# A two-layer graph network on one core: slabs 2 to 6 multiply a folded, re-split hT once in fp16, and the epilogue's operations stand in other steps

## The chip, the cores and the metric

The kernel runs on one core of one Trainium2 chip. The core has five engines, each with an instruction queue of its own that it works off in order: PE multiplies matrices, DVE and ACT work elementwise and read the results of PE out of PSUM, POOL works elementwise on SBUF and issues the large loads, SP issues the small ones. They wait for each other through semaphores. The metric is the time of one execution on the device, in microseconds (us).

## The reference

There are 4096 nodes with 64 features each (x) and a 0/1 matrix adj of 4096 x 4096 with about 16 ones in a row.

```python
# layer 0
support = x @ W0
rank = cumsum(adj, axis=1); deg = rank[:, -1:]
k = minimum(deg, 100)
w = adj * where(rank - (deg - k) > 0, 0.5 ** (k - (rank - (deg - k))), 0)   # the last neighbour counts 1, the one before 1/2, ...
x1 = layernorm(x + w @ support + b0)
# layer 1
deg1 = sum(adj, axis=1) + 1
z = concat([x1, (adj @ x1 + x1) / deg1]) @ W + b1      # W = [Wx; Wn]
o = relu(z)
out = layernorm(x1 + o / max(norm(o), 1e-12))
```

The layer norms have no weights; eps is 1e-5.

## The kernel before, in words

**Tiles.** The host hands over the adjacency transposed and cut into 64 tiles. Tile (g, k) holds the 512 rows of slab g (the destinations) and the 512 columns of chunk k (the sources); it comes as 1 MB of f32 and is written into SBUF as bf16, 512 KB (L105). There are 33 buffers for such tiles. Slab by slab, and within a slab from chunk 7 down to chunk 0, this gives the 64 steps of the main loop (L539 to L576): step 8g is the first of slab g. Eight loads are issued ahead; step i issues load i + 8, on POOL's queue.

**One step, layer 0.** For every tile the neighbours are counted with matmuls against `pick` (`count`, L248), the counts are added up on DVE (cs, L258 or L260), multiplied out to all ranks (`spread`: rep on PE, L266; near on ACT, L268), and turned into exponents v by two times 16 matmuls of 32 x 32 (`weigh`, L278 and L287). ACT makes one half of v into the weights w (L294), DVE the other (L295): the exponent is written as an integer whose bits are a bf16 power of two. PE then sums w times x over the tile (`gather`, acc, L305), one step later. The two halves of v fill PSUM tiles that exist once, so the v of a step waits for both w of the step before. Slabs 0 to 2 count and spread tile by tile; slab 3 first by one and then by two, slab 4 by two, slabs 5 and 6 by four, slab 7 by two, two and four. x is split into a high and a low fp16 half (`xhl`; the low one times 2048), so acc holds 64 rows of high and 64 rows of low sums: hT is [128, 512].

**The epilogue of a slab** runs in the steps of the next slab, spread over them by a table of hooks: `at(i, engine, fn, g)` puts a function at the end of step i on PE, DVE or POOL, ahead of that step's w (ACT), or behind it ("ACT, late"). Counting from the first step of the next slab: `first_hT` copies acc (ACT, L408); step 1 `first_pz`, four fp32 products hT times W0 (L414) and four degree matmuls (L416), and `first_y` (L421, L422); step 2 `first_mv` (mean and variance); step 3 `first_s` (root, ACT) and `first_r`; step 4 `first_x1` (four scalings on DVE, L441); step 5 `first_hi` (ACT, L446) and `first_xl` (DVE, L450); step 6 `first_lo` (ACT, L453), `first_px` (four transposes, PE, L458) and `first_least`; step 7 `first_x1T` (ACT, L461) and `first_pu` (x1 times Wx, eight fp16 matmuls, PE, L468); step 8 `first_c1` (DVE, L473 and L476: bias, times the degree). Functions on one engine and step run in the order of their registration.

**Sums of layer 1.** When a slab's x1hl is ready, adj times x1 can be summed for every tile in SBUF whose chunk that slab is. `jobs` lists 39 tiles that are summed within the loop, four matmuls a step (`some_sums`, QUOTA = 4, L314, into the one bank "acc1"); steps in SAVED make none. A finished job is copied (ACT) or added (DVE) into part (`evict_part`, L334, L337). The buffer of a tile comes free with its sum, so later loads wait on POOL for these sums.

**Other work on the queues.** In slab 0 ACT and POOL split x (`split_x`, L208, L210); POOL prepares the weights (L216 to L227), adds b0 to x (L238) and the identity to the diagonal tiles (`add_self`, L233).

**The tail** (L579 on) does the last slab's layer 0, the sums that are left and layer 1's epilogue in an order written out by hand; PE works through to about 207 us, then DVE, POOL and ACT end the chain.

The order of a step in the loop:

```python
            run(i, ACT)
            load_next()
            run(i, POOL)
            w = weigh(g, k, nr) if i == 0 else None
            for s in share:
                count(*s, s == ahead[0], s == ahead[-1])
            w = w or weigh(g, k, nr)
            run(i, "ACT, late")
            ...
            run(i, PE)
            run(i, DVE)
```

Of the kernel before, what the change touches and what calls it, by code (L numbers as in the profile page):

```python
# [9 lines left out]
F32 = mybir.dt.float32  # L10
BF16 = mybir.dt.bfloat16
FP16 = mybir.dt.float16
# [3 lines left out]
ALU = mybir.AluOpType  # L16
AX = mybir.AxisListType
PE = mybir.EngineType.PE
ACT = mybir.EngineType.Activation
DVE = mybir.EngineType.DVE  # L20
POOL = mybir.EngineType.Pool
SP = mybir.EngineType.SP

P = 128
R = 512
TB = R // P
KB = 4
# [3 lines left out]
W_EXP = 127 - MAX_NEIGH  # L31
LO = 2048.0
W_UP = 256.0
LN_EPS = 1e-5
L2_EPS = 1e-12
QUOTA = 4
SAVED = 23, 26, 28


@with_exitstack  # L40
def adj_resnorm_kernel(
# [23 lines left out]
    nc = tc.nc  # L65
    D = x.shape[2]
    NG, NK = adjT.shape[0], adjT.shape[1]
# [4 lines left out]
    const = ctx.enter_context(tc.tile_pool(name="const", bufs=1))  # L72
# [39 lines left out]
    c1 = const.tile([P, NB, D], F32, name="c1")  # L112
    xp = c1

    def load_xp(k0, k1):
        bs = slice(k0 * KB, k1 * KB)
        nc.sync.dma_start(out=xp[:, bs, :], in_=x_quads[:, bs, :])
# [33 lines left out]
    nc.vector.memset(eps_ln, LN_EPS)  # L151
    ident = epi.tile([P, P], F32, tag="near", name="ident")
    nc.vector.tensor_scalar(ident, dist, 0.0, None, ALU.is_equal)


    has = epi.tile([P, P], BF16, tag="y", name="has")
# [23 lines left out]
    nc.vector.memset(less, -STEP * MAX_NEIGH)  # L180


    wts = const.tile([P, 5 * D], F32, name="wts")
    w0_sb, wn_sb, wx_sb, b1_sb, b0_sb = [wts[:, j * D : (j + 1) * D] for j in range(5)]

    wx_parts = const.tile([P, 2, D], FP16, name="wx_parts")
    part = {}
# [17 lines left out]
    def split_x(k):  # L205

        bs = ts(k, KB)
        nc.scalar.copy(xhl[:, bs, 0:D], xp[:, bs, :])  # L208
        xrs[k] = epi.tile([P, KB, D], F32, tag="z", name=f"xr_{k}")
        nc.gpsimd.tensor_tensor(xrs[k], xp[:, bs, :], xhl[:, bs, 0:D], ALU.subtract)  # L210

# [11 lines left out]
    def prepare_wx():  # L223
        for rows, up in ((slice(0, D), W_UP), (slice(D, P), W_UP / LO)):
            nc.gpsimd.tensor_scalar(wx_sb[rows, :], wx_sb[rows, :], up, None, ALU.mult)
        nc.gpsimd.tensor_copy(wx_parts[:, 0, :], wx_sb)
        nc.gpsimd.tensor_tensor(wx_parts[:, 1, :], wx_sb, wx_parts[:, 0, :], ALU.subtract)  # L227

    def add_self(g):

# [13 lines left out]
    def count(g, k, first, last):  # L244
        if first:
            cnt[g] = ps_m.tile([P, R], F32, tag="m", name=f"cnt_{g}_{k}")
        for q in range(KB):
            nc.tensor.matmul(  # L248
                cnt[g][quarters[q], :],
                lhsT=pick[:, PW - 4 * k : PW - 4 * k + Q],  # L250
                rhs=A[g][k][:, q, :],
                start=first,
                stop=last,
            )
        if last:
            new = one.tile([P, R], BF16, tag="cs", name=f"cs_{g}_{k}")
            if g in cs:
                nc.vector.tensor_tensor(new, cnt[g], cs[g], ALU.add)  # L258
            else:
                nc.vector.tensor_copy(new, cnt[g])  # L260
            cs[g] = new
# [8 lines left out]
    def weigh(g, k, nr):  # L270

        w = wp.tile([P, KB, R], I16, tag="w", name=f"w_{g}_{k}")
        v = [ps_v.tile([P, 2, R], F32, tag="v", name=f"v_{g}_{k}_{i}") for i in range(2)]
        for q in range(KB):
            for e in range(4):
                nc.tensor.matmul(  # L278
                    v[e // 2][quarters[q], e % 2, :],
                    lhsT=tri[quarters[e], :],  # L280
                    rhs=A[g][k][quarters[e], q, :],
                    start=True,
                    stop=False,
                )
        for q in range(KB):
            for e in range(4):
                nc.tensor.matmul(  # L287
                    v[e // 2][quarters[q], e % 2, :],
                    lhsT=mine[quarters[e], 4 * k + q, :],
                    rhs=nr[quarters[e], :],  # L290
                    start=False,
                    stop=True,
                )
        nc.scalar.activation(w[:, 0:2, :], v[0], AF.Relu, bias=less)  # L294
        nc.vector.tensor_scalar(w[:, 2:4, :], v[1], -STEP * MAX_NEIGH, 0.0, ALU.add, ALU.max)  # L295
        return w
# [17 lines left out]
        nc.tensor.matmul(acc, lhsT=x1hl[:, b, :], rhs=A[g][b // KB][:, b % KB, :], start=first, stop=last)  # L314


    jobs = [(0, [0]), (1, [0])]
    jobs += [(2, [0, 1]), (0, [1]), (1, [1])]
    jobs += [(3, [1, 0, 2]), (0, [2]), (1, [2]), (2, [2]), (4, [2, 1, 0, 3])]
    jobs += [(0, [3]), (1, [3]), (2, [3]), (5, [3, 2, 1, 0, 4]), (3, [3, 4])]  # L320
    jobs += [(6, [4, 3, 2, 1, 0, 5]), (4, [4, 5]), (0, [4, 5]), (1, [4, 5]), (2, [4])]
    acc1 = {}

    todo = [(g, k * KB + q, (k, q) == (ks[0], 0), (k, q) == (ks[-1], KB - 1)) for g, ks in jobs for k in ks for q in range(KB)]
# [1 line left out]

    def ready(i, g, b):
        k = b // KB
        return i >= NK * (k + 1) + 7 and i >= when[g, k]

    def evict_part(g):
        acc = acc1.pop(g)
# [62 lines left out]
    def psum(n, m, name, dt=F32):  # L395

        if not banks:
            return ps_m.tile([P, n, m], dt, tag="m", name=name)
        bank = banks.pop(0)
        bank_of[name] = bank  # L400
        view = bank if dt == F32 else bank.bitcast(dt)
        return view[:, 0 : n * m].rearrange("p (n m) -> p n m", m=m)
# [1 line left out]
    bank_of = {}  # L404

    def first_hT(g):
        ep["hT", g] = epi.tile([P, R], F32, tag="hT", name=f"hT0_{g}")
        nc.scalar.copy(ep["hT", g], acc0[g])  # L408

    def first_pz(g):  # L410

# [25 lines left out]

    def first_x1(g):
        mv, y, r = ep["mv", g], ep["y", g], ep["r", g]
        for t in range(TB):  # L440
            nc.vector.tensor_scalar(  # L441
                x1[:, g * TB + t, :], y[:, t, :], mv[:, t, 0:1], r[:, t : t + 1], ALU.subtract, ALU.mult
            )

# [2 lines left out]

    def first_xl(g):
        xl = ep["xl", g] = epi.tile([P, TB, D], F32, tag="z", name=f"xl_{g}")
        nc.vector.tensor_tensor(xl, x1[:, ts(g, TB), :], x1hl[:, ts(g, TB), 0:D], ALU.subtract)  # L450

    def first_lo(g):
        nc.scalar.mul(x1hl[:, ts(g, TB), D : 2 * D], ep["xl", g], LO)  # L453
# [15 lines left out]

    def first_c1(g):  # L470

        t1 = c1[:, ts(g, TB), :]
        nc.vector.scalar_tensor_tensor(  # L473
            t1, ep["pu", g], 1.0 / W_UP, b1_sb.unsqueeze(1).to_broadcast([P, TB, D]), ALU.mult, ALU.add
        )
        nc.vector.tensor_tensor(  # L476
            t1, t1, deg[:, ts(g, TB)].unsqueeze(2).to_broadcast([P, TB, D]), ALU.mult
        )

    hooks = defaultdict(list)  # L480

    def at(i, engine, fn, *args):
        hooks[i, engine].append((fn, args))

    def run(i, engine):
        for fn, args in hooks.pop((i, engine), []):
            fn(*args)

    for k in range(NK):
        i = when[0, k]  # L490
# [6 lines left out]
    for g in range(NG):  # L497
        at(NK * g + 3, POOL, load_x, g)
        at(NK * g + 7, POOL, add_b0, g)
        at(min(NK * g + 12, NS - 2), POOL, add_self, g)  # L500
    for g in range(NG - 1):
        i = NK * (g + 1)
        at(i + 1, PE, first_pz, g)
        at(i + 1, DVE, first_y, g)
        at(i + 2, DVE, first_mv, g)
        at(i + 3, "ACT, late", first_s, g)
        at(i + 3, DVE, first_r, g)
        at(i + 4, DVE, first_x1, g)
        at(i + 5, ACT, first_hi, g)
        at(i + 5, DVE, first_xl, g)  # L510
        at(i + 6, ACT, first_lo, g)
        at(i + 6, PE, first_px, g)
        at(i + 7, ACT, first_x1T, g)
        at(i + 7, PE, first_pu, g)
        at(i + 6, DVE, first_least, g)
        at(i + 8, DVE, first_c1, g)

# [19 lines left out]
    for c, chunk in enumerate(chunks):  # L539
        ahead = chunks[c + 1] if c + 1 < len(chunks) else []  # L540

        shares = [[]] * (len(chunk) - 1) + [ahead]
        nr = near[chunk[0][0]]
        for (g, k), share in zip(chunk, shares):
            i = when[g, k]
# [4 lines that stand above are left out]
            w = weigh(g, k, nr) if i == 0 else None  # L550
            for s in share:
                count(*s, s == ahead[0], s == ahead[-1])
            w = w or weigh(g, k, nr)
            run(i, "ACT, late")
            if i == 0:
                warm(4)
            n_todo = len(todo)
            done = some_sums(i, 0 if i in SAVED else QUOTA)
            half = 0
            if share and share[-1] == ahead[-1]:  # L560
                if held is not None and len(todo) == n_todo:

                    half = KB // 2
                    gather(*held, 0, half)
                spread(*ahead[-1])
            if i == 0:
                warm(3)
            if done is not None:
                evict_part(done)
            if held is not None:  # L570
                gather(*held, half)
            held = (g, k, w)
            if g > 0 and k == NK - 1:
                first_hT(g - 1)
            run(i, PE)
            run(i, DVE)  # L576
# [317 lines left out]
```

## Time and profile before

| | us |
|---|---|
| median of 3 runs (236.61 to 238.28) | 236.71 |
| the profiled execution | 236.54 |
| its span, first to last instruction | 234.4 |
| PE busy | 210.6 (90%) |
| DVE busy | 180.1 (77%) |
| ACT busy | 136.6 (58%) |
| POOL busy | 82.6 (35%) |
| adjacency loads: 64 of 512 KB, median from issue to landing | 16.6 |
| main loop: first L278 of step 0, first L278 of step 63 | 12.4, 189.1 |

Busy times are sums over an engine's instructions; overlapping matmuls count once. The mean granted clock of PE is 0.978, and the page's row for it shows full speed in nearly every slice. A timeline's row has start, length, engine, line, operation, output<-input and shapes; "x16" are 16 instructions in one row, and in brackets stands how long the engine was idle before and what ended it. A waits row has the engine and line that waited, what for, the sum in us, how often, and the longest.

### The profile page before, as it was taken

What the parts mean: (1) busy time and instruction counts of PE and PEld (TensorE: products, weight loads), DVE (VectorE), ACT (ScalarE), POOL (GpSimd) and SP (SyncE); (2) the same over time, 40 slices, a digit from 0 to 9 for tenths busy, and PEclk for the clock granted to TensorE, in tenths of its full rate; (3) what the DMA queues carried; (4) which work ended last, traced back from release to release, by engine and by line L of the source; (5) the groups of instructions that cost most, each with busy time, mean ns of one, the idle gap of its engine ahead of it and who ended that gap; (6) DMA issues with size and microseconds to landing.
All of it is one profiled execution on the core that took longest, in us unless ns stands there. A gap on an engine that the chain in (4) does not pass through costs nothing.

```text
span 234.4 us, 7427 instructions
## 1 busy us (share of the span) xinstructions
PE 210.6 (90%) x3129; PEld 97.0 (41%) x3172; DVE 180.1 (77%) x461; ACT 136.6 (58%) x205; POOL 82.6 (35%) x158
## 2 busy tenths in 40 slices
PE   7689979889998999999999999999999999999920
PEld 2223324234434343453345334533443345676810
DVE  5459897987897779779857985597579776499983
ACT  6068877688678765665655555555565551232684
POOL 8334583432531330312231143114441000069970
PEclk9799999999999999999999999999999999999985
DMA  6999999999999999999999999999980000000013
GB/s 201 212 212 219 208 214 212 222 215 215 218 216 212 216 219 214 214 216 212 219 213 204 201 190 191 168 174 172 212 167 3 0 3 0 3 0 3 25 45 112
DMA packets 11985, 37.34 MB, mean 159 GB/s; under 512 B 1328, under 2 KB 3504, under 8 KB 11952
## 3 DMA queue, kind: packets, MB, share of 16 engines
q0 software_dynamic: 9216, 33.56, 73.4%
q1 hardware_dynamic: 2736, 3.31, 4.6%
q8 instruction: 25, 0.41, 0.6%
q14 instruction: 8, 0.07, 0.1%
HBM read 69.37 MB, written 1.05 MB: 300 GB/s over the span
## 4 chain that ended last, share of the span: by engine, by line
PE 50%; DVE 7%; POOL 4%; ACT 3%; issue 2%; ACTq 0%; POOLq 0%
PE acc L305 13%; PE acc_part L314 12%; PE v L278 6%; PE cnt L248 4%; PE v L287 3%; PE pz L414 2%; ACT u L788 2%; DVE w L295 2%; POOL scratch L774 2%; PE vb L314 2%; POOL scratch L805 2%; PE rep L266 1%; PE va L757 1%; DVE x L441 1%; PE va L314 1%
## 5 line engine op out<-in xcount | busy, mean ns | idle before, releaser
L294 ACT ACTIVATE w<-v,less 128x1024 int16<-128x1024 f32 x64 | 71.2, 1113 | 48.5 <-PE v L287 36.2
L295 DVE TENSOR_SCALAR w<-v 128x1024 int16<-128x1024 f32 x64 | 78.2, 1221 | 18.6 <-PE v L287 17.2
L105 POOL DMA_DIRECT2D a<-in_adjT_dram x64 | 35.4, 554 | 97.0 <-PE rep L266 35.4
L305 PE MATMUL acc<-w,xhl 128*128 128x512 bf16 x240 | 66.1, 379 | 2.1 <-issue 1.1
L314 PE MATMUL acc_part<-a,x1hl 128*128 128x512 bf16 x132 | 37.3, 381 | 2.1 <-issue 1.4
L305 PEld LDWEIGHTS <-xhl 128*128 128x128 f16 x256 | 23.0, 98 | 32.6 <-issue 9.3
L268 ACT ACTIVATE near<-rep,most 128x512 bf16<-128x512 f32 x40 | 27.3, 682 | 8.3 <-PE rep L266 8.2
L314 PEld LDWEIGHTS <-x1hl 128*128 128x128 f16 x224 | 18.5, 98 | 31.2 <-issue 13.8
L278 PE MATMUL v<-a,tri 32*32 32x512 bf16 x1024 | 28.6, 384 | 0.5 <-ACT w L294 0.5
L287 PE MATMUL v<-near,mine 32*32 32x512 bf16 x1024 | 27.8, 376 | 0.0
L248 PE MATMUL cnt<-a,pick 128*32 128x512 bf16 x256 | 21.4, 389 | 5.8 <-DMA a<-in_adjT_dram 4.2
L258 DVE TENSOR_TENSOR cs<-cnt,cs 128x512 bf16<-128x512 f32 x32 | 21.9, 684 | 5.4 <-PE cnt L248 5.1
L278 PEld LDWEIGHTS <-tri 32*32 32x32 bf16 x1024 | 9.6, 87 | 19.5 <-issue 18.7
L774 POOL TENSOR_TENSOR scratch<-scratch,power 128x4 f32<-128x4 f32 (+1 forms) x5 | 6.4, 1278 | 29.5 <-DVE scratch L776 29.4
L266 PE MATMUL rep<-cs,further 128*128 128x512 bf16 x40 | 15.4, 385 | 1.0 <-DVE cs L258 1.0
L248 PEld LDWEIGHTS <-pick 128*32 128x32 bf16 x256 | 5.9, 94 | 20.8 <-issue 12.4
L233 POOL TENSOR_TENSOR a<-a,ident_b 128x128 bf16<-128x128 bf16 x32 | 12.7, 429 | 0.1
L287 PEld LDWEIGHTS <-mine 32*32 32x32 bf16 x1024 | 10.5, 87 | 2.8 <-issue 2.6
L788 ACT ACTIVATE u<-u,scratch 128x64 f32<-128x64 f32 x27 | 9.8, 429 | 2.2 <-POOL scratch L807 2.1
L260 DVE CAST cs<-cnt 128x512 bf16<-128x512 f32 x8 | 5.5, 692 | 6.9 <-PE cnt L248 6.8
L446 ACT CAST x1hl<-x 128x256 f16<-128x256 f32 x8 | 3.2, 405 | 11.1 <-DVE x L441 9.2
L771 ACT ACTIVATE u<-u 128x256 f32<-128x256 f32 (+1 forms) x5 | 2.5, 502 | 12.1 <-DVE u L760 12.1
(134 smaller groups left out, 245.0 us busy)
## 6 DMA issues: line engine op xcount, KB each, us to landing
a<-in_adjT_dram POOLq DMA_DIRECT2D x64, 512.0 KB, 16.6
c<-in_x_quads_dram SPq DMA_DIRECT2D x2, 512.0 KB, 4.5
x<-in_x_dram SPq DMA_DIRECT2D x8, 128.0 KB, 7.6
out_dram<-u SPq DMA_DIRECT2D x8, 128.0 KB, 1.7
wts<-in_weights_dram SPq DMA_DIRECT2D x1, 160.0 KB, 7.1
```

The source lines that it names most:

```text
L105: nc.gpsimd.dma_start(out=a, in_=adjT[g, k])
L248: nc.tensor.matmul(cnt[g][quarters[q], :], lhsT=pick[:, PW - 4 * k : PW - 4 * k + Q], rhs=A[g][k][:, q, :], start=first, stop=last,)
L258: nc.vector.tensor_tensor(new, cnt[g], cs[g], ALU.add)
L266: nc.tensor.matmul(pr, lhsT=further, rhs=cs[g], start=True, stop=True)
L268: nc.scalar.activation(near[g], pr, AF.Relu, bias=most, scale=-1.0)
L278: nc.tensor.matmul(v[e // 2][quarters[q], e % 2, :], lhsT=tri[quarters[e], :], rhs=A[g][k][quarters[e], q, :], start=True, stop=False,)
L287: nc.tensor.matmul(v[e // 2][quarters[q], e % 2, :], lhsT=mine[quarters[e], 4 * k + q, :], rhs=nr[quarters[e], :], start=False, stop=True,)
L294: nc.scalar.activation(w[:, 0:2, :], v[0], AF.Relu, bias=less)
L295: nc.vector.tensor_scalar(w[:, 2:4, :], v[1], -STEP * MAX_NEIGH, 0.0, ALU.add, ALU.max)
L305: nc.tensor.matmul(acc0[g], lhsT=xhl[:, b, :], rhs=w[:, q, :].bitcast(BF16), start=(k, q) == (NK - 1, 0), stop=(k, q) == (0, KB - 1),)
L314: nc.tensor.matmul(acc, lhsT=x1hl[:, b, :], rhs=A[g][b // KB][:, b % KB, :], start=first, stop=last)
L788: nc.scalar.activation(o[:, t, :], y[:, t, :], AF.Identity, bias=off[:, t : t + 1], scale=r[:, t : t + 1])
```

## The change

For slabs 2 to 6 (`HALVED`) hT's low half is folded into its high half in f32 (`half_sum`, DVE), the sum is split again into an fp16 high part (`half_high`, ACT), what is left of it (`half_rest`, DVE) and that as fp16 low part (`half_low`, ACT), both in x1T. Eight fp16 matmuls of 128 columns (`half_pz`) then give hT times W0 and hT times W0·C·Wx side by side, with C the centring of the layer norm. With x·C·Wx and b0·C·Wx taken in the first 14 steps (`early_px`, `early_xT`, `early_pu`, `early_xw`), x1 times Wx follows by scaling with the norm's root and needs neither x1's transposes nor `first_pu`. The products of weights that this takes are made on PE and POOL in steps 6 to 10. The degree matmuls get a step of their own (`half_degree`).

`half_scale` (DVE), `half_b1`, `half_c1` and `half_c1_b1` (POOL) take the place of `first_c1`. In slabs 0 and 1 the product with the degree moves to POOL (`times_degree`); `first_x1` goes to POOL in slabs 0 to 3, `first_xl` in slabs 0, 1, 2, 4 and 6; the high cast of x goes to POOL in steps 2 to 7. Halved slabs run `first_mv` to `first_lo` a step later by default, and a table PLACES moves single operations; "DVE, early" is a new place ahead of a step's w. Sums become ready one step after `first_lo`; `jobs` names the same 39 tiles in another order, and SAVED is another list. Three of the 33 tile buffers serve as `prep` and `xTs` at first. The weights' load grows from 320 to 385 columns.

```diff
-SAVED = 23, 26, 28
+HALVED = range(2, 7)
+PLACES = {..., "first_mv 0": (10, "DVE, early"), "first_r 0": (11, "DVE, early"), "first_pu 0": (16, PE), "times_degree 0": (18, POOL), "first_pu 1": (24, PE), "half_high 2": (26, ACT), "half_rest 2": (26, DVE), "half_degree 2": (26, PE), "half_low 2": (27, ACT), "half_pz 2": (27, PE), "half_y 2": (27, DVE), "first_x1 2": (30, POOL), "first_xl 2": (31, POOL), "first_x1 3": (37, POOL), "first_hi 3": (38, "ACT, late"), "half_low 3": (34, ACT), "first_s 4": (44, ACT), "half_scale 4": (45, "DVE, early"), "first_xl 4": (46, POOL), "first_lo 4": (47, "ACT, late"), "half_low 4": (42, ACT), "half_b1 4": (46, POOL), "half_c1_b1 4": (46, POOL), "first_s 5": (52, ACT), "half_scale 5": (53, DVE), "first_hi 5": (54, "ACT, late"), "half_low 5": (50, ACT), "first_s 6": (60, ACT), "first_xl 6": (62, POOL), "first_lo 6": (62, "ACT, late"), "half_low 6": (58, ACT)}
+LAG = 1
+SAVED = (15, 17, 18, 21, 27)
...
+    prep = a16p.tile([P, KB * R // 2], F32, tag="a16", name="prep")
+    xTs = [a16p.tile([P, KB, R], FP16, tag="a16", name=f"xT_{j}") for j in range(2)]
...
-    wts = const.tile([P, 5 * D], F32, name="wts")
+    wts = const.tile([P, 6 * D + 1], F32, name="wts")
...
-        nc.scalar.copy(xhl[:, bs, 0:D], xp[:, bs, :])
+        (nc.gpsimd.tensor_copy if k < NK - 2 else nc.scalar.copy)(xhl[:, bs, 0:D], xp[:, bs, :])
...
+    def early_px(g):
+        ep["ex", g] = early_bank([P, R], FP16, f"ex_{g}")
+        for t in range(TB):
+            nc.tensor.transpose(ep["ex", g][:, ts(t, P)], xhl[:, g * TB + t, :], ident16)
+    def early_xT(g):
+        nc.scalar.copy(xT[g]..., ep["ex", g]...)
+    def early_pu(g):
+        pu = ep["eu", g] = early_bank([P, TB, D], F32, f"eu_{g}")
+        for t in range(TB):
+            for j in range(2):
+                nc.tensor.matmul(pu[:, t, :], lhsT=xT[g][:, ts(t, P)], rhs=wc_parts[:, j, :], start=j == 0, stop=j == 1)
+    def early_xw(g):
+        nc.vector.scalar_tensor_tensor(
+            c1[:, ts(g, TB), :], ep["eu", g], 1.0 / W_UP, b0c.unsqueeze(1).to_broadcast([P, TB, D]), ALU.mult, ALU.add
+        )
...
-        return i >= NK * (k + 1) + 7 and i >= when[g, k]
+        return i >= low_at[k] + LAG and i >= when[g, k]
...
+    def half_sum(g):
+        h = ep["hT", g]
+        nc.vector.scalar_tensor_tensor(h[0:D, :], h[D:P, :], 1.0 / LO, h[0:D, :], ALU.mult, ALU.add)
+    def half_high(g):
+        nc.scalar.mul(x1T[0:D, :], ep["hT", g][0:D, :], 2.0 ** (W_EXP - 1))
+    def half_rest(g):
+        h = ep["hT", g][0:D, :]
+        nc.vector.scalar_tensor_tensor(h, h, 2.0 ** (W_EXP - 1), x1T[0:D, :], ALU.mult, ALU.subtract)
+    def half_low(g):
+        nc.scalar.mul(x1T[D:P, :], ep["hT", g][0:D, :], LO)
+    def half_pz(g):
+        pz = ep["pz", g] = psum(TB, 2 * D, f"pz0_{g}")
+        for t in range(TB):
+            for j in range(2):
+                nc.tensor.matmul(pz[:, t, :], lhsT=x1T[:, ts(t, P)], rhs=wz_parts[:, j, :], start=j == 0, stop=j == 1)
+    def half_y(g):
+        ...
+        nc.vector.scalar_tensor_tensor(y, pz[:, :, 0:D], 2.0 / W_UP, x1[:, ts(g, TB), :], ALU.mult, ALU.add)
+        nc.vector.scalar_tensor_tensor(c, pz[:, :, D : 2 * D], 2.0 / W_UP, c, ALU.mult, ALU.add)
...
+        by = nc.gpsimd if g in [0, 1, 2, 3] else nc.vector      # first_x1
+        by = nc.gpsimd if g in [0, 1, 2, 4, 6] else nc.vector   # first_xl
...
+        all_at(NK - 2, (0, POOL, bias_columns), (0, PE, centered), (1, ACT, centered_out), (1, POOL, centered_parts),
+            (1, PE, products), (2, ACT, products_out), (2, POOL, products_parts))
+    for j, g in enumerate(reversed(HALVED)):
+        all_at(j + 3, (0, PE, early_px, g), (1, ACT, early_xT, g))
+        all_at(NK + 1 + j, (0, PE, early_pu, g), (0, DVE, early_xw, g))
...
+        late = 1 if g in HALVED else 0
+        all_at(i + late, (2, DVE, first_mv, g), (3, "ACT, late", first_s, g), (3, DVE, first_r, g), (4, easy, first_x1, g),
+            (5, ACT, first_hi, g), (5, easy, first_xl, g), (6, ACT, first_lo, g), (5, DVE, first_least, g))
+        if g in HALVED:
+            all_at(i, (0, DVE, half_sum, g), (1, "ACT, late", half_high, g), (1, DVE, half_rest, g),
+                (1, PE, half_degree, g), (1, DVE, half_degree_out, g), (2, "ACT, late", half_low, g), (2, PE, half_pz, g),
+                (2, DVE, half_y, g), (4, DVE, half_scale, g), (5, POOL, half_b1, g), (6, POOL, half_c1, g),
+                (7, POOL, half_c1_b1, g))
```

## The prediction

> **What bounds the kernel now.** I read the page's busy row and its 40 slices first, then stretches of about one slab, then the PE timeline of one epilogue, then the waits. One execution took 236.54 us, its span 234.4; 2.1 us lie around the span, and the median of the runs shown, 236.71, is 0.17 above it. Differences found in the span are therefore taken off 236.7.
>
> ```profile
> PE 210.6 (90%) x3129; PEld 97.0 (41%) x3172; DVE 180.1 (77%) x461; ACT 136.6 (58%) x205; POOL 82.6 (35%) x158
> ...
> PE   7689979889998999999999999999999999999920
> ...
> GB/s 201 212 212 219 208 214 212 222 215 215 218 216 212 216 219 214 214 216 212 219 213 204 201 190 191 168 174 172 212 167 3 0 3 0 3 0 3 25 45 112
> ```
>
> PE is full from slice 8 on. The load rate is flat near 215 GB/s through slice 20 (123 us) and falls after that: loading is at its limit in two thirds of the main loop, and from there PE sets the pace.
>
> ```profile
> core 0: us, PE busy (x) PEld busy (x) DVE busy (x) ACT busy (x) POOL busy (x), PEclk, DMA share, GB/s
> 23.04:54.67 31.63, 28.04 (x517) 11.39 (x521) 26.47 (x50) 24.24 (x35) 15.33 (x31) 1.00 1.06 215
> ...
> 125.05:148.57 23.52, 22.66 (x375) 10.00 (x380) 17.82 (x36) 12.68 (x16) 6.72 (x15) 1.00 1.03 194
> 148.57:171.82 23.25, 22.67 (x374) 9.89 (x378) 16.83 (x35) 13.12 (x17) 8.84 (x22) 1.00 1.02 183
> ```
>
> The first stretch is steps 4 to 15, the others are steps 41 to 48 and 49 to 56, with the epilogues of slabs 4 and 5. A step starts here with its first matmul of L278. In the late slabs PE lacks 0.6 to 0.9 us of being full; in the early stretch it lacks 3.6, and the waits of 24 to 54 us say for what:
>
> ```profile
> POOL a L105 <- DMA a<-in_adjT_dram: 11.8, 9, 2.2
> PEld L248 <- DMA a<-in_adjT_dram: 6.7, 10, 1.1
> ```
>
> The packets of the load queue, added up in order of their ends and cut at each 512 KB, give the landing of each of the 64 tiles: 2.46 us apart up to tile 46, some 2.8 where an x load comes between. No tile is counted (L248) less than 1.06 us after its landing; at tiles 8 to 15 this is 1.06 to 1.55, so steps 7 to 14 follow the loads. Tile 43 lands at 117.81 and is counted at 119.44, 1.63 later. That is a **wall**: step 39 (now at 119.77) can come no more than about 0.5 us sooner, whatever is saved ahead of it. From tile 47 on the distance is 3 us and more at the end of each chunk, and there PE time counts in full.
>
> Now one epilogue on PE (step 49):
>
> ```profile
> 148.57 0.43 PE L278 MATMUL v<-a,tri 32*32 32x512 bf16 x16
> 148.79 0.42 PE L287 MATMUL v<-near,mine 32*32 32x512 bf16 x16
> 149.15 1.04 PE L314 MATMUL acc_part<-a,x1hl 128*128 128x512 bf16 x4
> 150.02 1.03 PE L305 MATMUL acc<-w,xhl 128*128 128x512 bf16 x4
> 150.89 1.00 PE L414 MATMUL pz<-wts,hT 128*128 128x64 f32 x8
> 151.72 0.24 PE L416 MATMUL pz<-ones,cs 128*128 128x1 bf16 x4
> 151.90 0.43 PE L278 MATMUL v<-a,tri 32*32 32x512 bf16 x16
> ```
>
> It lasts 3.33 against 2.42 of step 48, so L414 and L416 cost 0.91 (0.83 and 0.18 by their starts, with 0.1 of a gap covered). Step 46, with 16 counting matmuls (0.98) and px, lasts 3.62: px costs 0.22. Step 47, with a rep (0.22) and pu, lasts 2.86: pu costs 0.22. Together **1.35 us a slab**.
>
> **The change, part by part.**
>
> *PE in slabs 2 to 6.* L414, px and pu go; the degree matmuls stay, alone in their step (0.18, of which 0.08 falls into the gap at the step's end); eight fp16 matmuls of 128 columns come. No such matmul is in the trace. Below it stands pu, eight of 64 columns in 0.32 (0.04 each), above it px, four of 128 columns with a weight load each in 0.31 (0.08 each). The form is px's, so 8 x 0.08 = 0.62, 0.54 after the gap; the ends are 0.24 and 0.62. Saved: 1.35 - 0.10 - 0.54 = **0.71 a slab**, between 0.63 and 1.01.
>
> *PE early.* Per halved slab four transposes (0.31) and eight 64-column matmuls (0.32) go into steps 3 to 7 and 9 to 13, with three small fp32 products (two passes each at the 0.104 of L414: 0.6). That is 3.8 us of PE. Cover: steps 4 to 15 hold 3.6 us without PE work because loads and chains are awaited. On ACT the five copies of xT (0.59 as L461, 2.9) stand against six casts of x that move to POOL (0.40 as L208, 2.4). On DVE five sums of 0.42 (as L473) come, 2.1, and for slab 0 the x1 group (1.00), xl (0.41) and the second c1 operation (0.42) go, 1.8. I take 0 at the wall; without the cover it is 3.8 in full.
>
> *DVE per halved slab.* Added: the fold and the rest, each two SBUF inputs of 64 x 512 f32, not in the trace. I take them by their 512 columns, as L710 and L777 (0.69); the lower end is L450 at 256 columns (0.41), the upper end 0.69 and a wait of up to 0.74 for POOL (below). Then a second sum behind y (0.42) and a small product (0.16). Removed: L473 and L476 (0.84), in places xl (0.41) and x1 (0.97). Net 0.3 less to 1.1 more in 23.5, where DVE is busy 17. The sum fits, the order need not: v's banks are one step deep, so a step can't end before DVE's w of the same step has, 0.66 + 1.22 after its start, and what stands ahead of w in DVE's queue adds to that. In step 41 the fold waits for hT (in step 49 this ended 0.70 after the step began): fold from 0.76 to 1.45, w to 2.70, next step at 2.75. PE alone would take 2.51, so the fold costs 0.24 in slabs 4 and 5. In slabs 2, 3 and 6 hT is ready 0.15 into the step, but the cs sum of the chunk (0.69) is queued behind the fold, and rep, near and the next v behind that: w from 1.6 to 2.85, next step at 2.95 against 2.72, again 0.23. The rest stands behind a part sum (0.68) in step 41 and pushes w of step 42 to 1.5; that step is 3.9 long, so it is hidden by the counting matmuls.
>
> *ACT.* half_high and half_low (0.58 each, by L408's 0.59) for x1T (0.59). half_low of slab 4 stands ahead of w in step 42, hidden likewise. first_s of slab 4 stands ahead of w in step 44: with y at the end of step 42 and a part sum and mv (0.96) in step 43, DVE reaches mv's end some 1.3 into step 44, s 0.29, w 1.11: the step takes 2.8, not 2.41. Cost 0.4. Slabs 5 and 6 have no part sum in that place: 0 to 0.1.
>
> *x1 and POOL.* In slab 4 PE now waits for x1:
>
> ```profile
> 136.33 1.79 DVE L441 TENSOR_SCALAR x<-y,mv_l,r_l 128x64 f32<-128x64 f32 x4
> ...
> 136.86 1.57 POOL L233 TENSOR_TENSOR a<-a,ident_b 128x128 bf16<-128x128 bf16 x4
> ```
>
> Four operations take 1.79 beside add_self, 0.97 elsewhere; hi and ACT's w follow, and step 45 lasts 2.86 instead of 2.41. The change puts x1 a step later, after add_self and ahead of the long step 46: 0.45 gained. The same in slab 6 (step 61, 2.65): 0.24. For slabs 0 to 3 x1 runs on POOL, four of about 0.4 (L225 0.37, L804 0.51) = 1.6, behind the load of its step, which waits for sums (issue about 2.1 into the step). hi is then due one step on, late in ACT's queue in step 38, so it still makes it; if not, ACT's w waits for POOL. POOL also takes xl, three c1 operations and times_degree, 0.74 each as L238: at most 1.6 + 4 x 0.74 = 4.6 beside 6 of 23.
>
> Moved to POOL, a sum of 256 columns takes 0.74 (L238) and not 0.42 (L476), and costs the path nothing while POOL idles two thirds of a slab. Where the two engines met, DVE was slow: the small L430 took 1.12 beside L238, 0.16 elsewhere. The c1 operations come in the fifth to eighth step and the folds in the first two, so I count 0; each meeting would cost up to 0.74.
>
> The Trainium skill speaks against this move in GPSIMD Engine Reference, section 4.1 (two-input sums on VectorE, being about twice slower on GpSimd): by that rule the sum is 0.3 to 0.4 us worse for each operation that the path has to wait for, by the row 0.32. Its page SBUF — State Buffer, Who interferes with whom, says that a DVE instruction with two SBUF inputs and a GpSimd instruction that reads SBUF lock each other out of a shared port pair; L430's 1.12 agrees, and by the rule the fold, the rest and the scaling all are such instructions, so a meeting in each of five slabs would make 3.7 us.
>
> *Loads and sums.* One weight load grows by 32 KB, 0.15 us of loading at 215 GB/s, within the wall's count. The same 39 pairs are summed, 156 matmuls, in another order; six groups of four by step 29 in both. By buffers freed, loads 41 to 44 are issued about a step later than now, against a backlog of three to four tiles (tile 43: issued 107.39, landed 117.81), so the queue stays full.
>
> **The sum.** Step 39 sooner by the wall: 0.4 (PE alone would give slabs 2 and 3 2 x 0.71 less that pu, 1.2). pu of slab 3 in step 39: 0.22. Slab 4: 0.71 + 0.45 - 0.24 - 0.4 = 0.52. Slab 5: 0.71 + 0.07 (step 53's excess over 2.41) - 0.24 = 0.54. Slab 6: 0.71 + 0.24 - 0.23 - 0.2 (hi ahead of w in step 62) = 0.52. The tail keeps its order; c1 of slab 6 leaves DVE where it waited anyway: 0. Sum 2.2, **234.5 us**. Its own range: 3 x 0.08 from the matmul's price and 0.9 if each of three slabs meets one more late w (0.3) upward, 3 x 0.30 and half a microsecond of smaller stalls downward: 233.1 to 235.6.
>
> **Rivals.**
> *No stalls:* fold, s and hi cost nothing and the fp16 matmuls take 0.05 each, 0.32 a slab after the gap. Then 3 x 0.93 + 0.76 (steps 45, 53, 61) + 0.62 = 4.2: **232.5**. For it: DVE is idle 6 us a slab. Against: its order above.
> *DVE is the new bound:* in slabs 4 to 6 the rest lies on the path too, 3 x 0.69 = 2.1 given back: **236.6**. For it: w ends last in the steps under 2.42. Against: the long step after it takes it up.
> *Early work is not covered (slower):* the 3.8 us on PE and DVE's 2.1 of early sums lengthen steps 3 to 13 in full. Less the 1.2 of slabs 2 and 3, step 39 comes 4.7 later; the later slabs give back 1.8: **239.6**; with PE's part alone 237.5. It turns slower than before once step 39 is later than 119.8 + 1.8 = 121.6. For it: steps 9 to 13 hold cs, w and a sum on DVE, 2.3 us, and in some y, mv or r. Against: the waits for loads there.
>
> **How the numbers follow.** Chances: forecast 0.56, no stalls 0.20, DVE 0.12, early work 0.12. About 1%, 2.4 us, is what a measurement of this kernel tells from no change. The forecast lies near that bound (234.3): 0.25 of its chance is faster, 0.31 within. No stalls is faster; DVE is within but for 0.01; early work is slower but for 0.03. Faster 0.45, same 0.45, slower 0.10. The range takes in no stalls and DVE and leaves out most of early work and the outer ends: 232.4 to 237.0.
>
> **What would show it.** Right: counting waits for loads up to step 38 and step 39 starts 119.2 to 119.8; step 41 near 2.75 with the fold ahead of w; step 45 at 2.4; eight fp16 matmuls in about 0.6. Wrong: step 39 after 121, PE in steps 41 to 63 waiting for w in most steps, or POOL's x1 ending after ACT wants it.

## The result, and the profile after

The changed kernel takes 233.67 us (median of 4 runs, 233.60 to 234.10) against 236.92 (4 runs, 236.61 to 238.28): the ratio is 0.9856, with a 95% interval of 0.9815 to 0.9896. The profiled span fell from 234.4 to 231.7. The page's rows that answer to those of before:

```profile
PE 209.5 (90%) x3138; PEld 95.2 (41%) x3178; DVE 182.2 (79%) x454; ACT 140.6 (61%) x212; POOL 112.3 (48%) x211
...
PE   7589999998998999999999999999999999999910
...
GB/s 201 209 213 219 215 216 213 217 217 214 215 219 212 214 214 223 211 214 214 218 217 207 200 183 210 204 195 181 205 168 4 3 0 0 3 0 1 23 45 113
```

PE is only 1.1 us less busy: what slabs 2 to 6 save on it, the early transposes and products largely spend. POOL took on 30 us. Loads still run near 215 GB/s through slice 20. Stretches of the changed kernel, steps 4 to 15 and then 41 to 48 and 49 to 56 (columns: stretch, length, busy time and count of PE, PEld, DVE, ACT, POOL, granted clock, DMA share, GB/s):

```profile
core 0: us, PE busy (x) PEld busy (x) DVE busy (x) ACT busy (x) POOL busy (x), PEclk, DMA share, GB/s
23.22:55.45 32.23, 30.07 (x565) 14.27 (x570) 27.38 (x49) 24.69 (x38) 21.29 (x46) 1.00 1.07 216
124.82:147.28 22.46, 21.91 (x363) 9.04 (x367) 17.89 (x37) 13.13 (x17) 9.36 (x19) 1.00 1.03 199
147.28:169.71 22.43, 22.01 (x363) 8.78 (x366) 16.78 (x34) 13.84 (x18) 9.10 (x21) 1.00 1.05 196
```

Slabs 4 and 5 lost 1.06 and 0.82 (23.52 and 23.25 before). The early stretch is 0.6 longer than before (32.23 against 31.63), and PE lacks 2.2 of being full there instead of 3.6. The waits of 24 to 54 us for loads have shrunk:

```profile
POOL a L109 <- DMA a<-in_adjT_dram: 3.9, 4, 1.5
```

These were 11.8, and PE's weight loads waited 6.7 more. Where the main loop stands, step by step (first L278 of before, first L351 of after, same instruction):

| step | before | after | later by |
|---|---|---|---|
| 7 | 30.64 | 31.07 | 0.43 |
| 15 | 51.48 | 53.36 | 1.88 |
| 25 | 79.52 | 81.06 | 1.54 |
| 33 | 101.93 | 101.42 | -0.51 |
| 39 | 119.77 | 119.77 | 0.00 |
| 49 | 148.57 | 147.28 | -1.29 |
| 57 | 171.82 | 169.71 | -2.11 |
| 63 | 189.09 | 186.54 | -2.55 |

The early work costs 1.5 us, slabs 2 and 3 earn it back by step 39, and everything that remains is earned after step 39. Another 0.2 comes in step 63, where slab 6's pu stood. PE's timeline of the epilogue shown of before, steps 49 and 50:

```profile
147.28 0.43 PE L351 MATMUL v<-a,tri 32*32 32x512 bf16 x16
147.50 0.42 PE L360 MATMUL v<-near,mine 32*32 32x512 bf16 x16
147.86 1.04 PE L387 MATMUL acc_part<-a,x1hl 128*128 128x512 bf16 x4
148.74 1.03 PE L378 MATMUL acc<-w,xhl 128*128 128x512 bf16 x3
149.60 0.24 PE L496 MATMUL pd<-ones,cs 128*128 128x1 bf16 x4
149.77 0.54 PE L351 MATMUL v<-a,tri 32*32 32x512 bf16 x16
...
152.19 0.61 PE L505 MATMUL pz<-wz_parts,x1T 128*128 128x128 f16 x8
152.73 1.05 PE L321 MATMUL cnt<-a,pick 128*32 128x512 bf16 x16
```

Step 49 lasts 2.49 instead of 3.33: the fp32 product is gone and the degree matmuls fill the gap at the end. Its place is taken by 0.54 of L505 in step 50, ahead of the counting. The row at 149.77 lasts 0.54 where 147.28 lasts 0.43: inside it the v of step 50 waits for DVE's w.

### The profile page after: what moved, and what is told of

The parts are those of the page before. It is cut to its first block, busy times and chain, and to the rows that moved or that the text cites. A ratio compares the mean times of both kernels' runs of the same rounds, so it can differ in the third digit from the quotient of the medians.

```text
span 231.7 us, 7494 instructions
## 1 busy us (share of the span) xinstructions
PE 209.5 (90%) x3138; PEld 95.2 (41%) x3178; DVE 182.2 (79%) x454; ACT 140.6 (61%) x212; POOL 112.3 (48%) x211
## 4 chain that ended last, share of the span: by engine, by line
PE 40%; DVE 11%; POOL 4%; ACT 3%; issue 2%; ACTq 0%; DVEq 0%; POOLq 0%
PE acc L378 12%; PE acc_part L387 11%; PE v L351 5%; PE cnt L321 3%; PE v L360 3%; ACT u L961 2%; POOL scratch L947 2%; DVE w L368 2%; POOL scratch L978 2%; DVE cs L331 1%; PE rep L339 1%; PE va L930 1%; PE pz L505 1%; PE vb L387 1%; DVE part L403 1%
## 5 line engine op out<-in xcount | busy, mean ns | idle before, releaser
L378 PE MATMUL acc<-w,xhl 128*128 128x512 bf16 x235 | 65.2, 380 | 1.9 <-issue 1.1
L109 POOL DMA_DIRECT2D a<-in_adjT_dram x64 | 36.9, 622 | 48.2 <-PE acc_part L387 25.4
L387 PE MATMUL acc_part<-a,x1hl 128*128 128x512 bf16 x140 | 38.2, 381 | 1.8 <-issue 1.3
L351 PE MATMUL v<-a,tri 32*32 32x512 bf16 x1024 | 29.6, 384 | 0.3 <-DVE w L368 0.2
L351 PEld LDWEIGHTS <-tri 32*32 32x32 bf16 x1024 | 9.5, 87 | 21.7 <-issue 21.5
L565 POOL TENSOR_SCALAR x<-y,mv_l,r_l 128x64 f32<-128x64 f32 x16 | 9.1, 575 | 12.4 <-DVE dr L516 6.4
```

The costliest lines, as they stand in the source:

```text
L109: nc.gpsimd.dma_start(out=a, in_=adjT[g, k])
L351: nc.tensor.matmul(v[e // 2][quarters[q], e % 2, :], lhsT=tri[quarters[e], :], rhs=A[g][k][quarters[e], q, :], start=True, stop=False,)
L378: nc.tensor.matmul(acc0[g], lhsT=xhl[:, b, :], rhs=w[:, q, :].bitcast(BF16), start=(k, q) == (NK - 1, 0), stop=(k, q) == (0, KB - 1),)
```

## The experiments

All times stand beside runs of the kernel before on the same chip; a ratio is to that kernel, the interval 95%. Profiled executions differ by up to 0.6 us before step 7 already, so steps are compared by their lengths; where starts are compared, the offset at step 7 is looked at first.

**Is there a wall at step 39, and what does the early work cost?** `e1_no_early`: the changed kernel without the early transposes and products.

```diff
-        all_at(j + 3, (0, PE, early_px, g), (1, ACT, early_xT, g))
-        all_at(NK + 1 + j, (0, PE, early_pu, g), (0, DVE, early_xw, g))
+        pass
```

> The kernel after without early_px, early_xT, early_pu and early_xw (x times C Wx is therefore missing from c1; everything else is issued). Theory, the wall: step 25 starts 1.5 to 1.9 us sooner than in the kernel after (81.06), but tile 43 still lands at about 117.9 and is counted at the earliest 1.06 later, so step 39 starts at 119.2 to 119.4 instead of 119.77 and the time is 0.4 to 0.5 under that of the kernel after: 233.2. Rival, no wall: the early work costs 1.6 to 1.9 and all of it comes back: 232.0. Second rival, the early work is covered by waits: 233.7, with step 25 where it was.

Measured: 233.68 us, ratio 0.9843 [0.9778, 0.9908]. Step 25 began 0.85 sooner than in the changed kernel, so the early matmuls are not free. But step 39 began at 120.06, 0.29 later. PE's timeline of that run, step 38:

```profile
117.94 0.83 PE L321 MATMUL cnt<-a,pick 128*32 128x512 bf16 x12
119.73 0.40 PE L321 MATMUL cnt<-a,pick 128*32 128x512 bf16 x4 [0.96 <-DMA a<-in_adjT_dram]
120.06 0.43 PE L351 MATMUL v<-a,tri 32*32 32x512 bf16 x16
```

Three tiles of the chunk are counted, and then PE waits 0.96 for the fourth, tile 43. Its packets ended at 117.86; it was counted 1.87 later. The profile has a second time for the same load, the landing that its semaphore shows (the view by issues gives "us from issue to landing"): issued at 108.93, landed 10.8 later, at 119.7, and the count follows at 119.73. So PE waited for this landing, and not for something behind it. The steps after it have the lengths of the changed kernel to 0.02 each, and so the end is the same. The wall is there, and harder than either theory had it: all 0.85 went into it, and the run is as long as with the work.

**Does POOL's add_self slow x1, and is that worth anything?** `e2_add_self_later`: the kernel before with add_self one step later.

```diff
-        at(min(NK * g + 12, NS - 2), POOL, add_self, g)
+        at(min(NK * g + 13, NS - 2), POOL, add_self, g)
```

> The kernel before with one edit: add_self a step later (13 instead of 12). Theory, shared port: the four x1 operations of slab 4 take 1.0 instead of 1.79, step 45 goes from 2.86 to 2.41 and step 53 from 2.48 to 2.42, and the time falls by 0.3 to 0.5, to 236.3. Rival: add_self now meets xl (two SBUF inputs) in the next step, xl takes 0.8 instead of 0.41, lo and ACT's w come later and the gain is under 0.1.

Measured: 236.80 us, ratio 1.0004 [0.9968, 1.0041]. In the steps the theory holds: step 45 lasts 2.42 instead of 2.86, step 53 2.42 instead of 2.48. From this run's timeline:

```profile
136.59 0.98 DVE L441 TENSOR_SCALAR x<-y,mv_l,r_l 128x64 f32<-128x64 f32 x4
...
139.54 0.81 POOL L233 TENSOR_TENSOR a<-a,ident_b 128x128 bf16<-128x128 bf16 x2
```

The same four operations took 1.79 beside add_self; apart from it they take 0.98. The rival did not come: xl, the next operation on DVE, still took 0.41, and add_self began behind it. Step 39 to step 63 is 0.52 shorter. Step 39 itself began 0.26 later, and half a microsecond is inside this measurement's interval, so the whole time doesn't confirm it.

**Does the fold lie on the path?** `e3_fold_twice`: the changed kernel with one more operation of the fold's size behind it (times 0, so the value stays).

```diff
     def half_sum(g):
         h = ep["hT", g]
+        nc.vector.scalar_tensor_tensor(h[0:D, :], h[D:P, :], 0.0, h[0:D, :], ALU.mult, ALU.add)
```

> The kernel after with half_sum issued twice, the second time with a factor of 0, in slabs 2 to 6. Theory, the fold is hidden with hardly any margin (in step 41 w of DVE ends 0.05 after PE could go on): each second fold lengthens steps 25, 33, 41, 49 and 57 by 0.5 to 0.65, 2.5 to 3.2 in all: 236.2 to 236.9. Rival, what is late is taken up by the long step after it (42, 50, 58): 0 to 0.6, 233.7 to 234.3.

Measured: 237.66 us, ratio 1.0031 [1.0004, 1.0059]; the changed kernel's is 0.9856. DVE's timeline in step 41 of this run, which began at 126.64:

```profile
127.36 0.68 DVE L481 SCALAR_TENSOR_TENSOR hT<-hT 64x512 f32<-64x512 f32 x1 [1.12 <-ACT hT L477]
128.08 0.68 DVE L482 SCALAR_TENSOR_TENSOR hT<-hT 64x512 f32<-64x512 f32 x1
128.69 1.21 DVE L368 TENSOR_SCALAR w<-v 128x1024 int16<-128x1024 f32 x1
```

The second fold starts 0.72 after the first, and steps 33, 42, 50 and 57 grew by 0.71 to 0.72, step 25 by 1.02 (the second fold itself took 0.98 there): 3.9 in all. In slabs 4 and 5 the growth stands in steps 42 and 50, not in 41 and 49: step 41 still ended 2.49 after its start, and the v behind it waited inside its own rows. So there is no room around the fold: 0.72 more on DVE lengthened each of these places by all of it. That the single fold costs little in slabs 4 and 5 doesn't follow from this run; it is read below from the lengths of their steps in the changed kernel. The time is above the expectation of 236.2 to 236.9, which had granted margin.

**What does an fp16 set cost?** `e4_pz_twice`: the eight matmuls of half_pz done twice.

```diff
-        for t in range(TB):
-            for j in range(2):
-                nc.tensor.matmul(pz[:, t, :], ...)
+        for _ in range(2):
+            for t in range(TB):
+                for j in range(2):
+                    nc.tensor.matmul(pz[:, t, :], ...)
```

> The kernel after with the eight fp16 matmuls of half_pz issued twice (the second set starts anew, so the values stay). Theory, PE sets the pace in slabs 3 to 6 and eight such matmuls cost 0.54: 4 x 0.54 + 0 to 0.54 in slab 2, whose step 27 has no sums, 2.2 to 2.7: 235.9 to 236.4. Rival, DVE's order sets steps 42, 50 and 58 and PE has room there: under 1.2, 234.9 at most.

Measured: 235.66 us, ratio 0.9951 [0.9923, 0.9979]. Steps 27, 34, 42, 50 and 58 grew by 0.44 to 0.45 each, and step 28 gave 0.18 back. PE's timeline of step 42 in this run:

```profile
130.86 1.06 PE L506 MATMUL pz<-wz_parts,x1T 128*128 128x128 f16 x16
131.85 1.05 PE L321 MATMUL cnt<-a,pick 128*32 128x512 bf16 x16
```

Sixteen take 0.99 to the next start, eight took 0.54: the second eight cost 0.45, 0.056 each with their weight loads. They are on the path in all five slabs. The time is a little under the 235.9 to 236.4 expected, because a second set costs less than the 0.54 of the first.

**Is it the new order rather than the halving?** `e5_places_only`: HALVED empty, only the new places of slabs 0 and 1 and the new order of sums. In slabs 2 to 5 the product with the degree runs on POOL here too; slab 6's, one POOL operation that falls behind the last step, is left out.

```diff
-EARLY = 3
-HALVED = range(2, 7)
+EARLY = 2
+HALVED = ()
+PLACES = {k: v for k, v in PLACES.items() if k.split()[-1] not in "23456"}
```

(x1 and xl run on POOL in slabs 0 and 1 only.)

> The kernel after with no slab halved and no early work: slabs 2 to 6 have the epilogue of before in its old steps, slabs 0 and 1 keep the new places (x1, xl and the second c1 operation on POOL), and so do jobs, SAVED and the casts of x. Theory, the halved epilogue is what shortens the loop behind the wall: from step 39 to step 63 it takes 69.3 as before (66.8 in the kernel after), step 45 lasts 2.86, step 39 starts at 119.2 to 119.9, the time is 236.2 to 236.9. Rival, the places do half of it: step 39 to 63 under 68.3 and the time under 235.7.

Measured: 236.92 us, ratio 0.9988 [0.9966, 1.0011]. Step 39 began at 120.41, later than the expected 119.2 to 119.9, and from there to step 63 the lengths are those of before, but for step 45 (2.49 instead of 2.86: x1 and add_self still overlap, but x1 took 1.41 instead of 1.79; why isn't shown). Step 25 is 0.27 late, of which 0.33 was there at step 7, and from step 25 to 39 the loop takes 40.62 instead of 40.25. So the new places and the new order of the sums cost 0.37 ahead of step 39 and win as much behind it, in step 45; on the whole they earn nothing. The halving is the source.

**Are slabs 2 and 3 worth halving, if a wall follows?** `e8_slabs_4_to_6`: HALVED from 4 only; slabs 2 and 3 keep the old epilogue in its default places, and two of the five early sets go.

```diff
-HALVED = range(2, 7)
+HALVED = range(4, 7)
```

> The kernel after with slabs 4 to 6 halved and slabs 2 and 3 as in the kernel before. Theory, slabs 2 and 3 earn what the early work costs: without them step 39 starts 0.8 to 1.4 later than in the kernel after (120.6 to 121.2), the steps behind it are unchanged, and the time is 234.5 to 235.1. Rival, the wall sets step 39 whatever comes ahead: 119.8 and 233.7.

Measured: 236.10 us, ratio 0.9955 [0.993, 0.9981]. Step 39 began at 121.38, 1.61 later than in the changed kernel (0.8 to 1.4 were expected): without their own saving, slabs 2 and 3 don't earn back the early work. Step 39 is 0.23 longer, with slab 3's pu in it. From step 40 on all lengths agree but one: step 46 lasts 4.70 instead of 3.39. Its end on PE:

```profile
143.08 0.83 PE L322 MATMUL cnt<-a,pick 128*32 128x512 bf16 x12
145.04 0.40 PE L322 MATMUL cnt<-a,pick 128*32 128x512 bf16 x4 [1.12 <-DMA a<-in_adjT_dram]
```

It is tile 51, the last of its chunk, and again a load. The expectation missed this, and its time of 234.5 to 235.1 with it. POOL issued that load 1.85 later than in the changed kernel (135.14 against 133.29), but PE was 1.84 later there too (step 46), so the late issue alone makes no wait. The load itself was slow: it landed 9.9 after its issue instead of 8.2, and the count began as soon as it had, at 145.04. Its packets ended 6.6 after the issue (6.45 in the changed kernel), so nearly all of the difference lies between the last packet and the landing, 3.3 against 1.7. Why that took longer I can't explain. The ten times of this kernel lie between 235.15 and 236.67 and the profiled one took 236.54; whether the wait is in every execution stays open.

**Is the fold better behind cs in step 57?** `e6_fold_behind_cs`:

```diff
+PLACES["half_sum 6"] = (57, "DVE, early")
```

> The kernel after with half_sum of slab 6 put behind cs in DVE's queue (step 57, ahead of w) instead of ahead of it. Theory, in step 57 the fold met add_self (0.92 instead of 0.68) and cs behind it made PE wait for rep: step 57 goes from 3.13 to 2.75 to 2.9 and the time to 233.4. Rival, the step is set by DVE's three operations in any order: 3.0 to 3.13, no change.

Measured: 233.47 us, ratio 0.9860 [0.9842, 0.9878]. DVE's timeline of the changed kernel in step 57 first, and POOL's in the same microseconds:

```profile
169.89 0.92 DVE L481 SCALAR_TENSOR_TENSOR hT<-hT 64x512 f32<-64x512 f32 x1 [1.10 <-ACT hT L477]
170.84 0.69 DVE L331 TENSOR_TENSOR cs<-cnt,cs 128x512 bf16<-128x512 f32 x1
171.45 1.22 DVE L368 TENSOR_SCALAR w<-v 128x1024 int16<-128x1024 f32 x1
```

```profile
168.69 1.58 POOL L306 TENSOR_TENSOR a<-a,ident_b 128x128 bf16<-128x128 bf16 x4
```

And DVE's in the experiment, where step 57 began 0.62 later:

```profile
170.45 0.69 DVE L331 TENSOR_TENSOR cs<-cnt,cs 128x512 bf16<-128x512 f32 x1 [1.05 <-PE cnt L321]
171.17 0.68 DVE L481 SCALAR_TENSOR_TENSOR hT<-hT 64x512 f32<-64x512 f32 x1
171.78 1.21 DVE L368 TENSOR_SCALAR w<-v 128x1024 int16<-128x1024 f32 x1
```

The fold takes 0.68 instead of 0.92, and rep no longer waits for a late cs; the run removes both at once and doesn't tell their shares apart. Step 57 lasts 2.71 instead of 3.13, step 58 3.96 instead of 3.83: net 0.29. In the time of the whole it can't be seen.

**Can the early products go where they cost nothing?** `e7_wall_and_fold`: e6, with early_pu and early_xw in steps 15, 17, 18, 20 and 21 and slab 4's x loaded later.

```diff
-        all_at(NK + 1 + j, (0, PE, early_pu, g), (0, DVE, early_xw, g))
+        all_at((15, 17, 18, 20, 21)[j], (0, PE, early_pu, g), (0, DVE, early_xw, g))
+PLACES |= {"half_sum 6": (57, "DVE, early"), "load_x 4": (38, POOL), "add_b0 4": (41, POOL)}
```

> The kernel of the run before with two more edits: early_pu and early_xw in steps 15, 17, 18, 20 and 21, which make no sums, instead of 9 to 13; and the x of slab 4 loaded in step 38 instead of 35 (b0 added in 41), so that its 128 KB don't go ahead of tile 43. Theory, the wall: step 25 starts 0.4 to 0.8 sooner than in the kernel after, tile 43 lands at 117.6 instead of 117.9, step 39 starts 0.2 to 0.4 sooner; with step 57 the time falls by 0.5 to 0.7, to 233.1. Rival, the early products cost as much where they now stand: step 25 at 81.0, step 39 at 119.8 and 0.3 from step 57 alone.

Measured: 233.39 us, ratio 0.9853 [0.9837, 0.9868]. Step 14 came 0.51 sooner than in the changed kernel and step 25 0.11 later: the rival was right, the products cost as much in the one place as in the other. Tile 43's packets ended 0.47 sooner (117.47) with the x load out of the way, but it landed at 119.3, hardly sooner than in the changed kernel (119.4), and PE came to it 0.2 after that: step 39 was at 119.87. Step 57 gains as in e6. This is the lowest time of all kernels here, but it can't be told from the changed kernel's.

## Why the prediction was right, and where its steps were not

The forecast of 2.2 us against a measured 2.7 in the span (3.2 by the medians) had the mechanism right: PE time saved behind the wall counts, time saved ahead of it doesn't. That the total came so near is in part luck: of its 2.2, 0.4 was to come up to step 39 and 1.8 behind it; measured were 0 and 2.8, two errors that offset each other. Term by term:

**PE per slab, 0.71.** Held: the set costs 0.54 at its place, as foreseen, the degree 0.08, and px and pu give 0.23 each. The second set of e4 costs only 0.45, so some 0.09 of the first comes once and not with each set; no run shows for what. The Trainium skill, in TensorE: Matmul & The Clock Gate, Back-to-back issue gap, gives about 81 ns for a 128-column matmul with its weight load in a stream, and 56 ns as the isolated gap. The measured 56 ns agrees with the second figure; by the first, each further set would be an estimated 0.65.

**Step 39 sooner by 0.4: failed, it came at the same time.** Two errors met. The early work was forecast at 0 and cost 1.54 at step 25: 0.85 is what e1 leaves out, 0.44 the products of weights in step 7 (e1's step 7 still lasts 2.89 against 2.45), and the rest is no more than the difference between executions. So the cover of load waits hid 2.5 of PE's 3.8, where I counted all as hidden. Slabs 2 and 3 earned 1.54 from step 25 to 39, against the 1.2 that I named; beside e8, where they are not halved, it is 1.92 (38.71 against 40.63), less what the new places cost.

And the wall was put too early. I took a load as landed when its packets had ended, and the wall from the shortest distance to a count that I had seen, 1.06 (tile 0, which I overlooked, has 0.75). But in e1, where PE did wait for tile 43, the distance was 1.87. The landing by the semaphore gives the wall directly: in the 40 places of the ten traces where the counting waited for a load, it began 0.04 after this landing each time. In the kernel before tile 43 was issued at 107.39 and landed 12.0 later, at 119.4; its count began at 119.44. In the changed kernel these are 109.78, 9.6, 119.4 and 119.45. The counting of that chunk and the step after it, before and after:

```profile
118.75 1.09 PE L248 MATMUL cnt<-a,pick 128*32 128x512 bf16 x16
119.77 0.43 PE L278 MATMUL v<-a,tri 32*32 32x512 bf16 x16
```

```profile
118.80 1.05 PE L321 MATMUL cnt<-a,pick 128*32 128x512 bf16 x16
119.77 0.43 PE L351 MATMUL v<-a,tri 32*32 32x512 bf16 x16
```

So the kernel before already stood at the wall, held up by some 0.05 inside its first row, and had none of the 0.5 of room that I gave it. The changed kernel's PE reached tile 43 just as it landed, which is chance. The landing lies between 119.3 and 119.8 in the ten traces, so step 39 can't start sooner than about 119.7 to 120.2. Nor did the counting wait for loads up to step 38, as I had it: in the changed kernel no wait for a load shows behind tile 7.

**pu of slab 3 in step 39, 0.22.** Measured 0.23.

**Slab 4, 0.52: mis-sized, measured 1.06.** The x1 stall in step 45 went as foreseen, 2.86 to 2.41. The 0.4 for first_s in step 44 did not come. The timeline of the changed kernel, all engines:

```profile
134.42 0.36 DVE L458 BATCH_NORM_AGGREGATE mv_l<-st_l 128x2 f32<-128x6 f32 x4
...
134.81 0.30 ACT L427 ACTIVATE s_l<-mv_l,eps_ln 128x4 f32<-128x4 f32 x1 [0.88 <-DVE mv_l L458]
...
135.02 1.09 ACT L367 ACTIVATE w<-v,less 128x1024 int16<-128x1024 f32 x1
...
136.42 0.43 PE L351 MATMUL v<-a,tri 32*32 32x512 bf16 x16
```

I had the group of mv end 1.3 us into step 44; it ended 0.8 into it (134.78 after 134.01), since mv begins in step 43 as soon as the part sum is done. s and w then follow, 0.3 ahead of the next v. And the 0.24 for the fold was too much:

```profile
125.54 0.68 DVE L481 SCALAR_TENSOR_TENSOR hT<-hT 64x512 f32<-64x512 f32 x1 [1.13 <-ACT hT L477]
126.15 1.21 DVE L368 TENSOR_SCALAR w<-v 128x1024 int16<-128x1024 f32 x1
...
127.31 0.54 PE L351 MATMUL v<-a,tri 32*32 32x512 bf16 x16
```

The fold has the foreseen length and starts where I put it, but w starts 0.07 before the fold ends, and the next v starts 0.05 before w ends. My chain of plain lengths gave 2.75 for step 41; it took 2.49. What is left shows in the lengthened v row, and in step 42, which grew by 0.68 where pz explains 0.54: the fold and the rest together cost at most 0.14 there.

**Slab 5, 0.54: mis-sized, measured 0.82.** The same: the fold took nothing that can be seen there (step 50 grew by 0.55, the price of pz alone).

**Slab 6, 0.52: measured 0.44 in steps 57 to 62 and 0.22 with pu of step 63.** In step 57 rep starts 1.87 after the step's start instead of 1.46. Here a cost came that I had set to 0: the fold and POOL's add_self meet, and the fold, with cs and rep right behind it, is 0.24 slower. The rest, some 0.17, is cs queued behind the fold, for which I had 0.23. e6 removes both. Slab 3 pays for the same order: in step 33 rep starts 1.78 after the step's start instead of 1.46; in slab 2, where hT was ready ahead of the step, it starts at 1.48. The 0.2 for hi ahead of w in step 62 did not come; that step fell from 2.64 to 2.41.

**x1 and sums on POOL.** An x1 operation took 0.57 there, not 0.4, four 2.3 instead of 1.6. In slab 3 the last one ended at 118.25, and hi began on ACT at 118.28, when w ahead of it was done: in time, with no room. So the larger price cost nothing.

**The rivals.** *No stalls* (232.5) was right in that first_s (slab 4) and hi (slab 6) cost nothing and the fold in slabs 4 and 5 next to nothing; it failed on the wall, on step 57 and on the price of the matmuls (0.54 where it had 0.32). *DVE is the new bound* needs the rest on the path; in slab 5 step 50 grew by the price of pz alone, so it isn't, yet e3 shows that the fold stands just at the edge of it. *Early work is not covered* had a quarter of its lengthening come true, 1.5 of 3.8 + 2.1, and slabs 2 and 3 paid it back.

## What to carry to other kernels

Find the places where a transfer sets the time before adding up savings: what is saved ahead of such a wall is worth nothing, and extra work ahead of it costs nothing until it reaches the wall, and from there in full. Take as landed what the load's semaphore says, and not the end of its bytes. A moved operation that costs nothing may still stand at zero margin; doubling it on the chip tells a free operation with room from one without. Chains of three or four instructions on one engine can run shorter than the sum of their lengths, so a stall of a quarter of a microsecond, worked out so, may not be there.

## What the runs showed of the hardware beyond that

- Consecutive DVE instructions can overlap: w starts 0.07 before the fold or cs ahead of it ends (126.15 against 126.22; 171.45 against 171.53). Not all do: a cs or a second fold behind a fold starts 0.03 to 0.04 after its end (170.84 against 170.81; 128.08 against 128.04 in e3).
- A DVE and a POOL operation that meet can slow one of them. In step 57 an operation of add_self was running when the fold began, 0.38 ahead of that operation's end, and the fold took 0.92 instead of 0.68. In step 25, shown below on both engines, the fold began first and POOL's sum took 1.10, where the same sum takes 0.61 in slab 0. The Trainium skill states this in SBUF — State Buffer, Who interferes with whom: whoever issues first holds the shared ports and the other blocks. Both rows agree in who pays, though the loss is smaller than the overlap: 0.24 of 0.38, and 0.49 of 0.63. A row of the kernel before doesn't fit by its start: a small DVE product (0.16 elsewhere) began ahead of POOL's sum, while POOL was issuing a load, and lasted to the sum's end. Start times alone don't tell who pays.

```profile
81.08 0.68 DVE L481 SCALAR_TENSOR_TENSOR hT<-hT 64x512 f32<-64x512 f32 x1
```

```profile
81.14 1.10 POOL L604 TENSOR_TENSOR c<-c,deg 128x256 f32<-128x256 f32 x1 [6.84 <-DVE c L597]
```

And the two of the kernel before:

```profile
95.04 1.12 DVE L430 TENSOR_TENSOR least<-least 128x4 f32<-128x4 f32 x1
```

```profile
95.39 0.74 POOL L238 TENSOR_TENSOR x<-x,wts 128x256 f32<-128x256 f32 x1
```

- A scaling of 128 x 64 f32 by two per-partition numbers takes 0.57 on POOL and 0.31 on DVE:

```profile
L565 POOL TENSOR_SCALAR x<-y,mv_l,r_l x16: 572/572/596, 44.5 to 117.7; 128x64 f32<-128x64 f32 x16
L565 DVE TENSOR_SCALAR x<-y,mv_l,r_l x12: 301/308/342, 138.4 to 184.6; 128x64 f32<-128x64 f32 x12
```

(count, then shortest, median and longest in ns, first and last start, shapes.)
- From the end of a tile's packets to the matmul that waits for it passed 0.75 to 1.95 us in these runs, and 3.31 in one place of e8; from the landing that the semaphore shows it was 0.04 each time. The packets were added up in order of their ends and cut at each 512 KB, so the first distance is as good as that cut. A wall computed from the shortest is placed too early.
